# Two attention layers on one core: the residual input loaded three beats ahead, and the reciprocals of the first element at the end of their beat

## The chip, the core and the metric

The kernel runs on one core of one Trainium2 chip. The metric is the device time of one execution in microseconds (us); lower is better. The time before is the median of three runs. One more execution was recorded by the hardware profiler, and all durations below are from it. TensorE (PE) does the matrix products, VectorE (DVE), ScalarE (ACT) and GpSimd (POOL) the elementwise work, SyncE (SP) starts the transfers, in the order of its program. PEld in the profile is TensorE's loading of weights.

## The reference

Two graph layers over x, eight elements of 2048 rows of 256 features, with one 2048 x 2048 adjacency matrix for all. Cut to what matters:

```python
# layer 0: attention, softmax within each chunk of 256 keys, 4 heads of 64
q, k, v = (x @ Wq.T + bq), (x @ Wk.T + bk), (x @ Wv.T + bv)      # split into heads
scores = clip(q . k / sqrt(64), -10, 10)                          # b h n j c, j = chunk
scores = where(mask == 0, -10, scores)
attn = softmax(scores, axis=-1)                                   # over the 256 keys of a chunk
ctx = einsum('bhnjc,bhjcd->bhnd', attn, vc)                       # summed over 8 chunks
out = layernorm(ctx @ Wo.T + bo + x) * gamma + beta
h = layernorm(x + out)
# layer 1: graph attention
Wh = h @ W;  e = leaky_relu(Wh @ a1 [:, None] + Wh @ a2 [None, :], 0.2)
attention = softmax(where(mask, e, -inf))
result = layernorm(h + elu(attention @ Wh))
```

## The kernel before

**Blocks and beats.** The queries of an element are worked on in four blocks of 512 rows (`ib`), the keys in tiles of 128 (`c`, 16 a block); two tiles are a chunk (`j`, 8 a block). One tile of keys against one block of queries is a *beat*: 16 beats a block, 64 an element, 512 for layer 0 in all. The order of instructions on every engine is that of the program; nothing reorders them. Each beat has the same frame:

- `begin_beat` starts the steps of layer 1 for the element before (from the second element on): `low`, `weights`, `leaky`.
- The scores of layer 0 (`sc`, L892, TensorE), their clip and mask on VectorE (L903), their exponentials on ScalarE (`e`, L907).
- The products of the chunk before (L961, TensorE): in an even beat the sums of exponentials (`u<-e,ones`) and one half of the values, in an odd beat the other half. ScalarE copies the halves to `un` (L969) and the sums to `ds` (L975).
- `end_beat`: the products of layer 1 (`us`, L749), then one step of each generator that is alive, and functions that an agenda holds for this beat.

**The way of a denominator.** `ds` holds the sums once for each of 32 rows; a transfer takes one row of each head into a narrow tile `dc` (L977). `inverse` takes its reciprocal on VectorE (L983) and stores it to `rd` in DRAM (L985); `spread` loads it back, spread over the rows, as `r` (L989). `scaled` multiplies `un` by `r` on VectorE (L996; L994 for the first chunk), and GpSimd adds the product to `ctxT` (L997). In the first element `inverse` and `spread` come one beat after the sums, an odd beat, and `scaled` three beats later, an even one; from the second element on, all come one or two beats after the sums at the end of an even beat. `un` has two buffers (one more in turns in the first element), so ScalarE's next copy into it waits until GpSimd has read the one before.

**The finish of a block** is the generator `fin`, started by `scaled` of one of the last chunks. It loads the block's rows of x (`x`, 512 KB, L349), makes `y` = x + bo and adds beta to x on GpSimd (L352, L353), waits until the last chunk is in `ctxT`, and then takes a step a beat: the output projection `po` (L360, TensorE) added to `y` (L367), statistics (L319, L320, L324 and GpSimd's L325), normalization (L332), gamma and the sum with x (GpSimd, L373, L374), a second normalization, the store of h, and its transposition (L386). The beats of `fin` are counted here from the block's first: before the change the load is issued in beat 15 and the additions in beat 16 of the block, that is, beside the next block's first beats; `po` comes in beat 19, in the first element in beat 21.

**What else runs in the first element.** Generators stand in the list ahead of the `fin`s: `projections` (keys and values of the elements, `pk`, `pv`), `weights_made`, `masks_made` and `far_made`. `masks_made` loads pieces of the adjacency matrix (L145) and makes two 8-bit masks of each (L154, L157, with L161 on the diagonal, on VectorE; L155 on ScalarE), and stores them (L190, L191). `far_made` loads rows of the matrix (L197) and makes the row masks of layer 1 (L201, L204), stored by L205. The queries of the next block are projected (`xT_q`, L120; `pq`, L256) at the end of beats 11 and 13 of a block in the first element, 13 and 15 in the others.

**From the second element on** `prelude` prepares layer 1 of the element before, on top of its steps: products `pw` (L401), and the row maxima of masked sums, `half_max` (L441, VectorE, from `sj_row` and a row mask `fb` that is loaded by L433 into the buffer just read).

In `end_beat`, as long as the beat is of the first element (`2 * NIB * NCH` is 64), the agenda's functions other than `scaled` run before everything else.

## Time and profile before

| | |
|---|---|
| runs | 4379.75, 4382.11, 4390.98 us; median 4382.11 |
| profiled execution | 4383.33 us; span 4381.5 us; mean granted TensorE clock 0.98 |
| TensorE busy | 4049.8 us, 92% |
| VectorE busy | 3386.4 us, 77% |
| ScalarE busy | 2555.5 us, 58% |
| GpSimd busy | 1761.7 us, 40% |
| transfers | 415.63 MB; all but 4 MB from SyncE's queue |

How to read it: busy times are unions over the profiled execution; an engine may be busy at a lower rate than its best. A line of the waits gives the waiting engine and its line, what it waited for, then the time in total, the number of waits and the longest. A line of the timeline gives the start in us from the span's start, the duration, the engine, the line, the operation, output and inputs by name, the shape, and in brackets the engine's idle time before it and what ended that. A line of the stretches gives the stretch and its length, then the busy time (and instructions) of PE, PEld, DVE, ACT and POOL, the granted clock, the busy share of the DMA engines and GB/s. The one who released a wait is inferred and can be wrong where several things were waited for.

### The profile page before, as it was taken

The numbers are of one execution on the slowest core, as the hardware profiler recorded it, in microseconds if no ns is written. First come the engines' busy times: TensorE is split into PE (matmuls) and PEld (weight loads), VectorE is DVE, ScalarE is ACT, GpSimd is POOL, SyncE is SP. The second block draws the span as 40 slices with busy tenths as digits, with TensorE's granted clock in tenths as the row PEclk, the third lists the DMA queues.
The fourth block names the chain that finished last, engine by engine and source line by source line (L and its number), as shares of the span: only waits on it lengthen the run. The fifth ranks groups of instructions, "written<-read, shape, count | busy, mean of one in ns | idle before, by whom it ended". The sixth has DMA issues, their size and how long they took to land.

```text
span 4381.5 us, 61169 instructions
## 1 busy us (share of the span) xinstructions
PE 4049.8 (92%) x23053; PEld 1914.0 (44%) x23053; DVE 3386.4 (77%) x4530; ACT 2555.5 (58%) x3842; POOL 1761.7 (40%) x901
## 2 busy tenths in 40 slices
PE   8898989999999999999899998999989999899767
PEld 3233334453345534454344543445434454344456
DVE  5775589966898668976689766996589965888777
ACT  5665556655566555666456665666556665555546
POOL 0332235533445434544245442554335542344420
PEclk9999999999999999999999999999999999999889
DMA  5554232223332233322333223232232222422321
GB/s 170 184 175 146 76 105 85 81 69 100 100 91 78 59 107 98 100 73 61 99 97 97 73 75 107 85 94 78 71 107 88 83 79 67 119 83 78 126 69 58
DMA packets 257641, 415.63 MB, mean 95 GB/s; under 512 B 85440, under 2 KB 120512, under 8 KB 256448
## 3 DMA queue, kind: packets, MB, share of 16 engines
q1 hardware_dynamic: 257344, 411.71, 30.9%
q8 instruction: 181, 2.97, 0.3%
q14 instruction: 116, 0.95, 0.1%
HBM read 340.66 MB, written 68.88 MB: 93 GB/s over the span
## 4 chain that ended last, share of the span: by engine, by line
PE 60%; DVE 20%; ACT 8%; DMA 6%; issue 5%; POOL 1%; SPq 0%; DVEq 0%; ACTq 0%; POOLq 0%
PE u L961 18%; PE sc L892 15%; PE us L749 12%; DVE sc L903 5%; DVE w L721 3%; DVE fb L441 3%; DMA dc<-ds 3%; ACT e L907 3%; PE pk L256 3%; PE pv L275 2%; PE pq L256 2%; PE po L360 2%; DVE w L726 2%; PE pw L401 2%; PE us L764 1%
## 5 line engine op out<-in xcount | busy, mean ns | idle before, releaser
L903 DVE SCALAR_TENSOR_TENSOR sc<-sc,mk 128x1024 f32<-128x1024 f32 x1024 | 1206.6, 1223 | 535.6 <-PE sc L892 390.1
L907 ACT ACTIVATE e<-sc 128x1024 f32<-128x1024 f32 x1024 | 1033.2, 1021 | 934.9 <-DVE sc L903 909.8
L892 PE MATMUL sc<-qT,kT 64*128 64x512 f32 x4096 | 1038.1, 622 | 60.5 <-ACT e L907 57.0
L997 POOL TENSOR_TENSOR ctxT<-ctxT,un 128x1024 f32<-128x1024 f32 x224 | 561.6, 2507 | 1078.1 <-DVE un L996 1053.3
L961 PE MATMUL u<-e,v 128*32 128x512 f32 x8192 | 981.4, 597 | 0.0
L749 PE MATMUL us<-wh,w 128*128 128x256 f32 x3584 | 880.0, 395 | 91.3 <-ACT w L730 69.6
L749 PEld LDWEIGHTS us<-wh,w 128*128 128x128 f32 x3584 | 667.9, 193 | 433.1 <-ACT w L730 121.3
L739 POOL TENSOR_TENSOR acc<-acc,w 128x512 f32<-128x512 f32 x392 | 600.7, 1533 | 550.4 <-ACT w L730 540.0
L892 PEld LDWEIGHTS sc<-qT,kT 64*128 64x128 f32 x4096 | 345.3, 187 | 572.0 <-issue 319.0
L721 DVE SCALAR_TENSOR_TENSOR w<-ab,sj,w 128x512 f32<-128x512 f32 x512 | 578.1, 1150 | 5.7 <-ACT w L717 5.6
L961 PEld LDWEIGHTS u<-e,v 128*32 128x32 f32 x8192 | 240.5, 110 | 656.8 <-issue 504.2
L961 PE MATMUL u<-e,ones 128*32 128x512 f32 x4096 | 496.5, 603 | 0.0
L726 DVE TENSOR_TENSOR w<-w,mk 128x512 f32<-128x512 f32 x512 | 459.7, 919 | 44.1 <-DMA mk<-mask 41.5
L441 DVE CUSTOM_DVE_ANT_0 fb<-sj_row,fb 128x1024 bf16<-128x1024 f32 x240 | 379.8, 1593 | 5.6 <-DMA fb<-far 5.4
L969 ACT COPY un<-u 128x512 f32<-128x512 f32 x512 | 300.8, 588 | 125.5 <-PE u L961 96.9
L717 ACT ACTIVATE w<-ab,sj 128x512 f32<-128x512 f32 x512 | 352.3, 715 | 11.4 <-POOL acc L737 5.4
L730 ACT ACTIVATE w<-w 128x512 f32<-128x512 f32 x512 | 308.8, 629 | 82.7 <-DVE w L726 82.2
L996 DVE TENSOR_TENSOR un<-un,r 128x1024 f32<-128x1024 f32 x224 | 279.1, 1246 | 43.5 <-DMA r<-rd 36.8
L961 PEld LDWEIGHTS u<-e,ones 128*32 128x32 f32 x4096 | 107.3, 109 | 350.4 <-issue 281.9
L983 DVE RECIPROCAL dc<-dc 128x16 f32<-128x16 f32 x256 | 63.9, 250 | 161.3 <-DMA dc<-ds 149.0
L360 PE MATMUL po<-WT_o,ctxT 128*128 128x256 f32 x512 | 128.7, 408 | 36.4 <-POOL ctxT L997 35.5
L975 ACT COPY ds<-u 128x512 f32<-128x512 f32 x256 | 148.6, 580 | 17.6 <-PE u L961 16.0
(112 smaller groups left out, 3059.8 us busy)
## 6 DMA issues: line engine op xcount, KB each, us to landing
r<-rd SPq DMA_DIRECT2D x256, 256.0 KB
mk<-mask SPq DMA_DIRECT2D x120, 512.0 KB
fb<-far SPq DMA_DIRECT2D x240, 256.0 KB
xT_k<-in_xT_dram SPq DMA_DIRECT2D x32, 512.0 KB
raw<-in_adjT_dram SPq DMA_DIRECT2D x32, 512.0 KB
rawf<-in_adj_dram SPq DMA_DIRECT2D x32, 512.0 KB
x<-in_x_dram SPq DMA_DIRECT2D x32, 512.0 KB
h_d<-y SPq DMA_DIRECT2D x32, 512.0 KB
```

The source lines that it names most:

```text
L441: nc.vector.tensor_tensor_reduce(out=fb, in0=row, in1=fb, scale=1.0, scalar=2 * FAR * 0.999, op0=ALU.add, op1=ALU.max, accum_out=dst,)
L717: nc.scalar.activation(self.w, k["ab"][:, 1, :], AF.Identity, bias=k["sj"][:, 1, c : c + 1])
L721: nc.vector.scalar_tensor_tensor(self.w, k["ab"][:, 0, :], k["sj"][:, 0, c : c + 1], self.w, ALU.add, ALU.max)
L726: nc.vector.tensor_tensor(self.w, self.w, self.k["mks"][self.c // HT][:, self.c % HT, :], ALU.min)
L730: nc.scalar.activation(self.w, self.w, AF.Exp)
L739: nc.gpsimd.tensor_add(k["acc"], k["acc"], self.w)
L749: nc.tensor.matmul(k["us"][:, t, :], self.w[:, ts(t, P)], k["wh"][c // TPB][:, c % TPB, 0:F], start=(first and t % 2 == 0), stop=last, ski ...
L892: nc.tensor.matmul(sc[:, h, :], kTs[b][n // TPB][h * D : (h + 1) * D, hp, ts(n % TPB, P)], qTs[b, ib][h * D : (h + 1) * D, hp, :], start=True,
L903: nc.vector.scalar_tensor_tensor(sc, sc, -CLIP, cap, ALU.max, ALU.min)
L907: nc.scalar.activation(e, sc, AF.Exp)
L961: nc.tensor.matmul(m[h * DH : (h + 1) * DH, :], prev["v"][pc // TPB][:, pc % TPB, f0 : f0 + DH] if part < 2 else ones[:, 0:DH], prev["es"] ...
L997: nc.gpsimd.tensor_add(p["ctxT"], p["ctxT"], p["un"])
```

## The change

The load of x is issued two beats earlier in the block (the chunk whose `scaled` starts `fin` moves by one), and `fin` yields three times instead of once between load and additions, which so keep their beat. In `end_beat`, the part for the first element is dropped: `inverse` and `spread` now run where `scaled` runs, after the products and after all generators of the beat, in the order in which they were entered.

```diff
@@ fin
         xt = one.tile([P, TPB, F], F32, tag="x", name=f"x{b}_{ib}")
         nc.sync.dma_start(out=xt, in_=x[b, ts(ib, IB), :].rearrange("(t p) f -> p t f", p=P))
-        yield
+        for _ in range(3):
+            yield
         y = one.tile([P, TPB, F], F32, tag="y", name=f"y{b}_{ib}")
         nc.gpsimd.tensor_add(y, xt, bc_rows(bo_bc))
         nc.gpsimd.tensor_add(xt, xt, bc_rows(beta_bc))
@@ end_beat
         nonlocal weighted
-        if beat < 2 * NIB * NCH:
-
-            now = agenda.pop(beat, [])
-            agenda[beat] = [fn for fn in now if fn.__name__ == "scaled"]
-            for fn in now:
-                if fn.__name__ != "scaled":
-                    fn()
-        elif beat >= 2 * total:
+        if beat >= 2 * total:
             for fn in agenda.pop(beat, []):
                 fn()
         for s in weighted:
@@ scaled
-                            if p["j"] == NCH - (4 if p["b"] == 0 else 3):
+                            if p["j"] == NCH - (5 if p["b"] == 0 else 4):
                                 fins.append(fin(p["b"], p["ib"], p["ctxT"]))
```

## The prediction

> **What bounds the kernel now.** First the page: its span and the engines' busy line. Then the stretches, cut where an element begins (an element has 64 beats).

> ```profile
> span 4381.5 us, 61169 instructions
> PE 4049.8 (92%) x23053; PEld 1914.0 (44%) x23053; DVE 3386.4 (77%) x4530; ACT 2555.5 (58%) x3842; POOL 1761.7 (40%) x901
> ```
> ```profile
> 0.00:453.50 453.50, 409.24 (x2384) 147.40 (x2384) 298.04 (x407) 258.61 (x334) 110.29 (x52) 0.97 0.52 164
> 970.00:1498.00 528.00, 502.12 (x2887) 237.82 (x2885) 416.67 (x544) 314.50 (x477) 233.02 (x121) 0.99 0.29 87
> ```

> TensorE bounds nearly everything: in the third element it idles 528.0 - 502.1 = 26 us of 528. A change off TensorE can win only such idle time, so I looked for the stalls that the moved instructions cause. The waits, over the whole run and then over the first 453.5 us:

> ```profile
> POOL y L352 <- DMA x<-in_x_dram: 106.6, 9, 15.7
> PE po L360 <- POOL ctxT L997: 35.5, 15, 4.2
> ```
> ```profile
> ACT un L969 <- POOL ctxT L997: 24.0, 4, 12.5
> DVE dc L983 <- DMA dc<-ds: 26.4, 13, 5.2
> PE pk L256 <- ACT un L969: 10.2, 1, 10.2
> ```

> GpSimd waits for x, and what is queued behind its two additions is the addition into ctxT, for which ScalarE (the buffer of un) and TensorE (po) wait. The timeline at the last block of the first element shows the whole chain:

> ```profile
> 425.45 0.42 SPq L349 DMA_DIRECT2D x<-in_x_dram  x1
> 426.42 1.22 DVE L996 TENSOR_TENSOR un<-un,r 128x1024 f32<-128x1024 f32 x1
> 432.81 2.34 POOL L352 TENSOR_TENSOR y<-x,bo_bc 128x1024 f32<-128x1024 f32 x1 [11.31 <-DMA x<-in_x_dram]
> 435.22 2.34 POOL L353 TENSOR_TENSOR x<-x,beta_bc 128x1024 f32<-128x1024 f32 x1
> 437.52 2.34 POOL L997 TENSOR_TENSOR ctxT<-ctxT,un 128x1024 f32<-128x1024 f32 x1
> 439.89 0.59 ACT L969 COPY un<-u 128x512 f32<-128x512 f32 x1 [12.45 <-POOL ctxT L997]
> 440.53 3.73 PE L256 MATMUL pk<-xT_k,WT_k 128*128 128x512 f32 x4 [10.16 <-ACT un L969]
> ```

> The product un was ready at 427.6; its addition began at 437.5, behind x. The second effect is at the first block of the third element:

> ```profile
> 1078.52 2.36 POOL L352 TENSOR_TENSOR y<-x,bo_bc 128x1024 f32<-128x1024 f32 x1 [14.62 <-PE sc L892]
> 1080.01 1.96 DVE L441 CUSTOM_DVE_ANT_0 fb<-sj_row,fb 128x1024 bf16<-128x1024 f32 x1
> 1080.96 3.24 POOL L353 TENSOR_TENSOR x<-x,beta_bc 128x1024 f32<-128x1024 f32 x1
> 1081.90 3.39 DVE L441 CUSTOM_DVE_ANT_0 fb<-sj_row,fb 128x1024 bf16<-128x1024 f32 x1
> 1088.11 1.23 DVE L441 CUSTOM_DVE_ANT_0 fb<-sj_row,fb 128x1024 bf16<-128x1024 f32 x1 [0.54 <-DMA fb<-far]
> 1094.16 2.07 PE L360 MATMUL po<-WT_o,ctxT 128*128 128x256 f32 x4 [3.63 <-POOL ctxT L997]
> ```

> The row maximum takes 1.23 us alone, and 1.96 and 3.39 beside the two additions. (The name PE sc in the first line is wrong: the scores were long done; the transfers of x end at 1078.4.)

> **Part 1, x earlier.** The condition on j moves by one chunk (two beats) and two yields are added, so the additions keep their beat, 16 of a block, and the load goes from beat 15 to 13. Nothing is added but waiting room. The additions then start when GpSimd is through with the ctxT addition of beat 14.

> *First element, block 3.* That addition ends at 421.5, x landed long before (7.4 us from issue to use in the rows), so the additions run 421.5 to 426.2. There they meet L201 and L204 of the far rows (422.8, 423.5); the second comes free at 426.2, the clips go from 424.1 to 426.7, un from 426.4 to 429.1, the ctxT addition ends at 432.7, and the copy of un starts there instead of at 439.9: 7.1 us won. Ends: 5, and 10 for the whole stall.
> *Block 2.* The additions (322.6 to 327.4) stretched mask operations from 0.63 and 0.68 to 2.38 and 2.84 us, and TensorE stalled 1.40 + 0.78. At the new place, 311.4 to 316.2, they delay clips by 2.3 us, of which about 0.5 gets through to the scores of 318.3: 1.7 won.
> *Block 1.* Stalls of 1.19 + 1.31; at the new place (216.7 to 221.4) one L201 is late, 0.9 us, and the scores at 223.3 don't need it: 2.5 won. Blocks 1 and 2 together: 1 to 4.7.
> *Block 0.* Stalls of 1.65 + 0.75 = 2.4 go. But the new place, 120.6 to 125.3, is where beats 15 and 16 make masks: five operations without any slack in front of the clips at 122.8. Each addition holds up one of them by up to 2.2 us (2.84 - 0.68); the clips come 4 us late, of which I take 3.0 as a new stall: -0.6 (ends -2.5 and 2.4).
> Sum: 7.1 + 1.7 + 2.5 - 0.6 = 10.7.

> [...]

> *Elements 1 to 7, first block (7 times).* The additions move from 1078.5 to about 1063.9, where VectorE idles for 6.45 us waiting for scores. The row maxima shrink by (1.96 - 1.23) + (3.39 - 1.23) = 2.9 us. Then fb is late next: the third maximum waited 0.54 us for it already, and its load is issued only when the first maximum is done. So at least 0.7, at most 2.9 at po; the transfer of dc, no longer behind x, adds about 1 us in two of the seven (at 2139.2 and 3730.9 the reciprocal waited 3.9 and 4.1 us for it, against 2.2 in the third element). I take 1.9, between: 7 x 1.9 = 13.3. All TensorE stalls around these seven places add up to 35.
> *At nothing.* Second and fourth blocks: the additions wait for no x there (idle before them 0.0), GpSimd's queue sets their start. Third blocks: they start 3.7 us earlier and free 2.2 us of VectorE, but L602 then waits for pr of TensorE until 1329.4 as now; without that cover 1.3 a block would be won. x now leaves just ahead of xT_q, which has 17.3 us (1048.6 to 1065.9) for what takes about 7; SyncE's 0.45 us an issue lie in its waits for ds. The buffer of x was last read at least five beats earlier.

> **Part 2, the reciprocals.** In the first element's 31 odd beats the reciprocal L983, its store rd and the spread r went first in the beat; now they stand behind masks, projections, far rows and all their loads and stores, on VectorE and on SyncE's queue. Nothing is removed; what changes is who waits. VectorE waited 26.4 us for dc, 13 times, with masks behind. Where masks or far rows were behind such a wait (145.0, 192.1, 286.3, 337.1), the clips came 1.74, 1.76, 2.07 and 1.9 us later than they would with the masks in the wait, and TensorE stalls followed (0.58 and part of 1.94 at po; 2.69; 4.86; 0.98). I take 1.2 + 1.8 + 2.0 + 1.0 = 6.0, ends -2 and 9. On SyncE the loads of an odd beat no longer wait for rd and r, and leave some 3 to 7 us earlier. r leaves 2 to 3 us later: of block 1's beat 31 it left at 219.2 for a product at 236.5, so it has some 15 us; if that cover were gone, every us would go to un at 31 places. Where SyncE waits for rd, dc of the next beat is queued: 1.5 us of room (r at 123.5, dc at 125.6).

> **Sum.** 10.7 + 13.3 + 6.0 = 30.0. The profiled execution took 4383.3 us (span 4381.5), 1.2 over the median of the three runs, so 4353.3. Lower ends 5 + 1 - 2.5 - 2 + 5 = 6.5; upper 10 + 4.7 + 2.4 + 9 + 25 = 51.

> **Rivals.** A measurement of this kernel can tell 0.3%, 13 us.
> *The collisions only move* (0.18). The additions meet other operations at their new places and blocks 0 to 2 lose what they win; fb lets only 0.7 x 7 = 5 through; part 2 gives nothing. 7.1 + 5 - 4 = 8 won: 4375. For it: ten operations of VectorE stand at the four new places of the first element; against it: the idle 6.45 us in the later elements. [...]
> *All stalls go* (0.13): the upper ends, 51 won: 4332.
> *The reciprocal takes the clips with it* (0.14). It is now the last thing before the clips of the next beat, with no mask work left to fill a wait for dc. If SyncE, behind the stores that wait for masks, sends dc so late that the wait hits the clips in all 31 beats by 1.5 us, that is +46 against part 1's 24: 4406, slower. It decides from a dc later by more than the masks' own 2.6 us (120.3 to 122.9) plus the 1.5 us of room; against it, the loads ahead leave earlier.
> *Forecast* (0.55): 4353. Doing something else than it says I exclude: the beats follow from the code. Faster is forecast and upper rival, 0.68; same 0.18; slower 0.14. The range 4334 to 4376 leaves out the slow rival and the far end of the upper one.

> **What would show it.** GpSimd's wait for x near 0 instead of 106.6; the copy of un behind ctxT (24.0) down to some 8, with the 10.16 stall at about 3; row maxima of 1.2 us throughout at first blocks, and po's 35.5 at about 20; mask operations of over 2 us at beats 15 and 16 of block 0; L983's waits for dc in the first 64 beats well below 26.4. It is wrong if L903 waits for L983 beat after beat, if xT_q or fb become waits, or if the first element ends less than 10 us earlier than 453.5.

## The result, and the profile after

The changed kernel takes 4358.92 us (median of six runs, 4357.85 to 4361.75), the kernel before, beside it on the same chip, 4379.36 us (4376.92 to 4390.98). The ratio is 0.9949, with an interval of 0.9939 to 0.9960: faster by 20.4 us. The forecast was 30.0 us off the profiled execution, to 4353 (4334 to 4376). The sign and the range held, and so did the mechanism at the longest stall; the gain of elements 1 to 7 did not come, and the terms of the first element's other blocks are not borne out. The time is 6 us off, but the gain nearly 10: the 30.0 were taken off an execution 4 us above the median of before, which hid the rest by luck.

The profiled execution of the changed kernel took 4357.91 us. Of its page, the span and the engines; of its stretches, the first element and the third, cut again where an element begins:

```profile
span 4356.1 us, 61109 instructions
PE 4044.4 (93%) x23053; PEld 1915.6 (44%) x23053; DVE 3378.8 (78%) x4530; ACT 2556.2 (59%) x3842; POOL 1755.6 (40%) x901
```
```profile
0.00:436.20 436.20, 403.17 (x2388) 146.65 (x2389) 302.10 (x407) 257.84 (x334) 110.64 (x52) 0.99 0.53 170
950.80:1479.30 528.50, 502.26 (x2887) 237.88 (x2885) 416.54 (x544) 314.84 (x477) 230.82 (x121) 0.99 0.29 87
```

The first element is 17.3 us shorter (436.2 for 453.5), and in it the granted clock rose from 0.97 to 0.99. The third element, where the forecast expected 1.9 us, is no shorter: 528.5 for 528.0. The two spans differ by 25.4 us, 5 more than the medians, because the one profiled execution of before lies 4 us above its median and that of the change 1 below; stretches of single profiles are read with that in mind. (A second profile of the change, taken with later runs, has a first element of 444.6 us, only 8.9 shorter.)

The waits, over the whole run (three lines) and then over the first element, 0 to 436.2 us (two lines):

```profile
PE po L361 <- POOL ctxT L991: 44.9, 17, 5.1
DVE fb L442 <- DMA fb<-far: 22.0, 8, 3.8
DVE dc L977 <- DMA dc<-ds: 140.7, 104, 4.7
```
```profile
DVE dc L977 <- DMA dc<-ds: 19.5, 10, 4.5
ACT un L963 <- POOL ctxT L991: 3.2, 1, 3.2
```

GpSimd's wait for x (106.6 us before) has no line any more. The copy of un behind ctxT fell from 24.0 to 3.2 us in the first element. But TensorE's wait for ctxT at `po` rose from 35.5 to 44.9, and VectorE's wait for `fb` came up from 5.4 to 22.0 us: of the prediction's own signs of being wrong, "if xT_q or fb become waits" has come for `fb`.

The timeline at the last block of the first element, the chain that the prediction showed:

```profile
395.89 0.90 SPq L349 DMA_DIRECT2D x<-in_x_dram  x1
...
412.99 2.37 POOL L353 TENSOR_TENSOR y<-x,bo_bc 128x1024 f32<-128x1024 f32 x1
414.18 1.73 DVE L201 TENSOR_SCALAR mf<-rawf 128x1024 bf16<-128x1024 int32 x1
415.44 2.70 POOL L354 TENSOR_TENSOR x<-x,beta_bc 128x1024 f32<-128x1024 f32 x1
415.95 2.27 DVE L204 TENSOR_TENSOR mf<-mf,off_h 128x128 bf16<-128x128 bf16 x1
...
420.56 1.21 DVE L990 TENSOR_TENSOR un<-un,r 128x1024 f32<-128x1024 f32 x1
421.91 2.34 POOL L991 TENSOR_TENSOR ctxT<-ctxT,un 128x1024 f32<-128x1024 f32 x1 [3.76 <-DVE un L990]
424.28 0.59 ACT L963 COPY un<-u 128x512 f32<-128x512 f32 x1 [3.24 <-POOL ctxT L991]
424.92 1.98 PE L256 MATMUL pk<-xT_k,WT_k 128*128 128x512 f32 x4 [1.84 <-ACT un L963]
```

x is issued 17 us before its additions, for a transfer that took 7.4 us before; nothing waits for it. The additions meet L201 and L204 as forecast (1.73 and 2.27 us long), and GpSimd is idle again when the product un comes. The stall of 10.16 us has become 1.84.

The first block of the third element, where two effects were to be seen, a gain and what comes after it:

```profile
1045.27 2.35 POOL L353 TENSOR_TENSOR y<-x,bo_bc 128x1024 f32<-128x1024 f32 x1
1047.70 2.34 POOL L354 TENSOR_TENSOR x<-x,beta_bc 128x1024 f32<-128x1024 f32 x1
1060.61 0.46 SPq L140 DMA_DIRECT2D mk<-mask  x1
1060.85 1.21 DVE L442 CUSTOM_DVE_ANT_0 fb<-sj_row,fb 128x1024 bf16<-128x1024 f32 x1
1061.99 1.22 DVE L442 CUSTOM_DVE_ANT_0 fb<-sj_row,fb 128x1024 bf16<-128x1024 f32 x1
1062.10 1.47 SPq L434 DMA_DIRECT2D fb<-far  x2
1069.05 1.23 DVE L442 CUSTOM_DVE_ANT_0 fb<-sj_row,fb 128x1024 bf16<-128x1024 f32 x1 [3.56 <-DMA fb<-far]
1072.70 2.34 POOL L991 TENSOR_TENSOR ctxT<-ctxT,un 128x1024 f32<-128x1024 f32 x1 [13.44 <-DVE un L990]
1075.10 6.46 PE L361 MATMUL po<-WT_o,ctxT 128*128 128x256 f32 x16 [4.67 <-POOL ctxT L991]
```

The gain is there: the row maxima take 1.21 and 1.22 us where they took 1.96 and 3.39. And it is lost again in the line of the third maximum, which waits 3.56 us for its rows `fb`, where it waited 0.54. The stall at `po` is 4.67 us, longer than the 3.63 of before. Just ahead of `fb` on the queue, at 1060.61, stands the load `mk` of the masks of layer 0, 512 KB.

### The profile page after: what moved, and what is told of

Read it like the earlier page. It is cut to its first block, busy times and chain, and to the rows that moved or that the text cites. A ratio compares the mean times of both kernels' runs of the same rounds, so it can differ in the third digit from the quotient of the medians.

```text
span 4356.1 us, 61109 instructions
## 1 busy us (share of the span) xinstructions
PE 4044.4 (93%) x23053; PEld 1915.6 (44%) x23053; DVE 3378.8 (78%) x4530; ACT 2556.2 (59%) x3842; POOL 1755.6 (40%) x901
## 3 DMA queue, kind: packets, MB, share of 16 engines
q1 hardware_dynamic: 257344, 411.71, 30.9%
## 4 chain that ended last, share of the span: by engine, by line
PE 58%; DVE 22%; ACT 7%; DMA 6%; issue 5%; POOL 1%; SPq 0%; DVEq 0%; ACTq 0%; POOLq 0%
PE u L955 18%; PE sc L886 14%; PE us L750 12%; DVE sc L897 6%; DVE w L722 3%; DVE fb L442 3%; PE pk L256 3%; PE pv L275 3%; ACT e L901 2%; DMA dc<-ds 2%; PE po L361 2%; PE pq L256 2%; PE pw L402 2%; DVE w L727 2%; PE us L765 1%
## 5 line engine op out<-in xcount | busy, mean ns | idle before, releaser
L750 PEld LDWEIGHTS us<-wh,w 128*128 128x128 f32 x3584 | 667.5, 193 | 426.4 <-ACT w L731 114.7
L722 DVE SCALAR_TENSOR_TENSOR w<-ab,sj,w 128x512 f32<-128x512 f32 x512 | 591.2, 1176 | 5.8 <-ACT w L718 5.8
L727 DVE TENSOR_TENSOR w<-w,mk 128x512 f32<-128x512 f32 x512 | 441.4, 883 | 45.0 <-DMA mk<-mask 42.5
L718 ACT ACTIVATE w<-ab,sj 128x512 f32<-128x512 f32 x512 | 352.2, 714 | 10.7 <-POOL acc L738 5.5
L361 PE MATMUL po<-WT_o,ctxT 128*128 128x256 f32 x512 | 133.9, 420 | 45.8 <-POOL ctxT L991 44.9
L969 ACT COPY ds<-u 128x512 f32<-128x512 f32 x256 | 148.5, 580 | 15.0 <-PE u L955 13.7
```

Source lines behind the costliest of these rows:

```text
L718: nc.scalar.activation(self.w, k["ab"][:, 1, :], AF.Identity, bias=k["sj"][:, 1, c : c + 1])
L722: nc.vector.scalar_tensor_tensor(self.w, k["ab"][:, 0, :], k["sj"][:, 0, c : c + 1], self.w, ALU.add, ALU.max)
L727: nc.vector.tensor_tensor(self.w, self.w, self.k["mks"][self.c // HT][:, self.c % HT, :], ALU.min)
L750: nc.tensor.matmul(k["us"][:, t, :], self.w[:, ts(t, P)], k["wh"][c // TPB][:, c % TPB, 0:F], start=(first and t % 2 == 0), stop=last, ski ...
```

## The experiments

Theory: the first element wins what its terms say, and elements 1 to 7 win little, since `fb` waits behind `mk`. Rivals: the parts are mis-sized in the first element; or `fb` is late because its load is issued late, whatever stands ahead of it.

**Only x earlier.** `end_beat` stays as before.

```diff
-        if beat >= 2 * total:
+        if beat < 2 * NIB * NCH:
+            now = agenda.pop(beat, [])
             ...
+        elif beat >= 2 * total:
```

> Only the early load of x (with the chunk that starts fin); the reciprocals of the first element stay first in their beat. Theory (the parts add up, as the prediction summed them): the whole change won 20 us by the medians, of which the reciprocals are 6, so this kernel is about 14 us faster than before, ratio 0.9967, and the stall of 10 us at the last block of the first element is gone here too. Rival (the load alone does it all): the whole 20 us, ratio 0.995. Second rival (the early load needs the later reciprocals, since raw loads hold up x): x still arrives late at GpSimd and no more than 5 us are won.

Measured: 4365.28 us against 4379.11, ratio 0.9971 (0.9961 to 0.9981), 13.8 us won, as expected. The 10-us stall is gone here too. From the sums of exponentials (`u<-e,ones`) of beat 64 to those of beat 66, across the stall, TensorE gains 9.0 us on the kernel before. But it starts those of beat 64 4.4 us later than the kernel before, so the first element is only 4.6 us shorter in this profile (448.9 for 453.5).

**Only the reciprocals later.** `fin` and its start stay as before.

```diff
-        for _ in range(3):
-            yield
+        yield
...
-   if p["j"] == NCH - (5 if p["b"] == 0 else 4):
+   if p["j"] == NCH - (4 if p["b"] == 0 else 3):
```

> Only the reciprocals behind the beat's other work in the first element; x is loaded one beat ahead of its additions as before. Theory: 6 us faster than before (ratio 0.9986); the clips after masks come earlier by 1.7 to 2.1 us where VectorE waited for dc, and the stall of 10 us behind x stays. Rival (the reciprocal takes the clips with it, dc late in every odd beat): slower by up to 20 us, ratio 1.005. Second rival (hidden anyway): 0 +- 2 us.

Measured: 4363.95 us, ratio 0.9963 (0.9950 to 0.9975), 15.2 us won, far over the 6.0 of the prediction. The timeline at the last block of the first element, with the code of x unchanged, shows what the 6.0 had left out:

```profile
416.82 0.43 SPq L349 DMA_DIRECT2D x<-in_x_dram  x1
420.91 2.35 POOL L352 TENSOR_TENSOR y<-x,bo_bc 128x1024 f32<-128x1024 f32 x1 [6.58 <-DMA x<-in_x_dram]
...
428.00 0.59 ACT L962 COPY un<-u 128x512 f32<-128x512 f32 x1 [7.74 <-POOL ctxT L990]
428.64 3.78 PE L256 MATMUL pk<-xT_k,WT_k 128*128 128x512 f32 x4 [5.44 <-ACT un L962]
```

x, too, is loaded in an odd beat, by a generator, so it too now goes ahead of `rd` and `r` on SyncE. The stall is 5.44 us instead of 10.16. Both parts take from the same stall: across it TensorE gains 9.0 us with the early x alone, 3.8 with the reciprocals alone and 8.9 with both, so that 3.9 us are counted twice when the parts are added up. Alone the parts win 13.8 + 15.2 = 29.0 by the medians, together 20.4; the other 4.7 us of the difference lie within the intervals of the medians (each some 5 us to either side). Added to the first part, the second wins 4365.3 - 4358.9 = 6.4, close to the prediction's 6.0, but good to some 6 us only.

**x earlier in the first element alone,** both parts of the change there, the later elements as before:

```diff
-        for _ in range(3):
+        for _ in range(3 if b == 0 else 1):
...
-   if p["j"] == NCH - (5 if p["b"] == 0 else 4):
+   if p["j"] == NCH - (5 if p["b"] == 0 else 3):
```

> The change, but x is loaded three beats ahead in the first element only; from the second element on it is loaded one beat ahead, as before. Theory after reading the changed kernel's trace (the leads of TensorE grow by 4 us in all over the first blocks of elements 1 to 7): this kernel is 4 to 8 us slower than the full change, so 12 to 16 us faster than before, ratio 0.9968. Rival (the prediction's term): 13.3 us slower than the full change, ratio 0.998.

Measured: 4362.93 us, ratio 0.9962 (0.9950 to 0.9975), 16.2 us won. The prediction had 10.7 + 6.0 = 16.7 for just this. In its profile the first element itself is 12.2 us shorter (441.3). For the elements 1 to 7 it leaves 4362.9 - 4358.9 = 4 us, where 13.3 was forecast; by the two intervals (each some 5 us to either side) the 4 is good to about 7.

**The mask loads of layer 0 two beats later.** The change, with the load of `mk` moved out of the way of `fb`:

```diff
-                if c % HT == 1:
+                if c % HT == 3:
```

> The change, and the loads of layer 0's mask blocks (512 KB, in beats 1 and 9 of a block) are issued two beats later, in beats 3 and 11, so that in the first block of an element they no longer stand ahead of the row masks fb. Theory (fb is held up by the mask load ahead of it on the same DMA rings): VectorE's wait of 3.6 us for fb at the first blocks falls below 1.5 us, po's stall there from 4-5 to 2-3 us, and the kernel is 8 to 16 us faster than the change, ratio 0.992 to before. Rival (fb is held up by r, the spread of the reciprocals, which lands on few of the rings, or by its own length): the wait stays within 1 us and so does the time.

Measured: 4318.06 us, ratio 0.9859 (0.9846 to 0.9873), 41 us below the change itself, where 8 to 16 were expected. The timeline at the same first block of the third element:

```profile
1058.55 1.22 DVE L442 CUSTOM_DVE_ANT_0 fb<-sj_row,fb 128x1024 bf16<-128x1024 f32 x1
1058.66 1.47 SPq L434 DMA_DIRECT2D fb<-far  x2
1062.62 1.22 DVE L442 CUSTOM_DVE_ANT_0 fb<-sj_row,fb 128x1024 bf16<-128x1024 f32 x1 [0.56 <-DMA fb<-far]
1068.68 3.72 PE L361 MATMUL po<-WT_o,ctxT 128*128 128x256 f32 x16 [1.69 <-POOL ctxT L991]
1068.72 0.47 SPq L140 DMA_DIRECT2D mk<-mask  x1
```

With `mk` behind it, `fb` is used 3.96 us after its issue (1058.66 to 1062.62); with `mk` ahead it took 6.95 us (1062.10 to 1069.05). The issue is not late, the transfer is: this separates the theory from its rival. The stall at `po` falls from 4.67 to 1.69.

**What early x is worth once the masks are out of the way.** The same one-line edit on the version with early x in the first element alone, and on the kernel before, and the change once more beside them (these three against 4379.41; the 4362.9 and the 4318.1 of the table are from above, against 4379.11):

> Mask loads two beats later, as in mask_two_beats_later, but x loaded three beats ahead in the first element only. Theory (the 13.3 us that the prediction put on the first blocks of elements 1 to 7 were swallowed by the wait for fb, and appear once fb is there in time): 10 to 14 us slower than mask_two_beats_later's 4318, so 4328 to 4332, ratio 0.989. Rival (an earlier x is worth 4 us there whatever fb does): 4322, ratio 0.987.

> The kernel before with nothing but the mask loads two beats later. Theory (early x and a free fb need each other in the later elements, the rest of the mask loads' gain is their own): the change is worth more on top of it than on top of the kernel before, 28 to 32 us instead of 20, so this runs in 4347 to 4350, ratio 0.993. Rival (independent): 41 us faster than before, 4338, ratio 0.9906.

> The change itself, beside the kernels of this call. The medians of its two parts alone, 13.8 and 15.2 us, add up to 29, the whole had won 20.4. Theory (in the first element the parts add up, 4.6 and 11.0 us of lead against 17.4 together, and the excess of the medians is scatter between runs): 20 us again, ratio 0.9954. Rival (the first measurement of the whole was low): 27 to 29 us, ratio 0.9935.

| early x | masks as they were | masks two beats later |
|---|---|---|
| nowhere (kernel before) | 4379.4 | 4354.2 (ratio 0.9942, 0.9929 to 0.9954) |
| first element only, with the reciprocals | 4362.9 | 4342.3 (0.9914, 0.9901 to 0.9926) |
| everywhere (the change) | 4358.9 (0.9953, 0.9941 to 0.9966) | 4318.1 (0.9859, 0.9846 to 0.9873) |

The change wins 20.5 us again, so its first measurement was not low. The other two miss what was expected of them: 4342.3 for 4328 to 4332, and 4354.2 for 4347 to 4350. Down the right column, early x in elements 1 to 7 is worth 4342.3 - 4318.1 = 24 us (good to some 8); down the left one, 4.

The traces show that this happens at the seven first blocks. Take from each later element the stretch from the first product of the sums in beat 14 to that in beat 26, and add up the seven; in it, take TensorE's waits at the scores (`sc`) for ScalarE's exponentials, and at `po` for ctxT (all in us, one profile each):

| kernel | stretch | wait at `sc` | wait at `po` |
|---|---|---|---|
| before | 542.4 | 24.5 | 24.5 |
| only the reciprocals later | 533.3 | 21.3 | 21.1 |
| x early in the first element only | 536.7 | 24.1 | 21.8 |
| only x earlier | 534.0 | 12.9 | 29.9 |
| the change | 538.0 | 13.6 | 30.5 |
| the change once more | 537.9 | 13.5 | 30.9 |
| before, masks later | 532.6 | 23.5 | 19.5 |
| x early in the first element only, masks later | 536.1 | 26.1 | 17.9 |
| the change, masks later | 513.2 | 12.6 | 15.0 |
| the change, third buffer | 526.1 | 13.6 | 24.2 |
| the change, both | 509.8 | 13.2 | 11.1 |

With the masks as they were, early x takes some 10 us off the wait at `sc` and puts most of it back at `po`; the stretch is as long as without. With the masks later it is some 20 us shorter. So the gain is real, and in the change it is used up by the wait for `fb`. Of the 41 us of the later masks, 24.8 lie in these stretches, and 13.7 in beats 26 to 38 (721.9 to 708.2), where the kernel before gains much the same from the masks alone (721.1 to 710.3).

With the masks later but x late, the maxima stand beside the additions again (x only in the first element early, third element):

```profile
1063.28 2.01 DVE L442 CUSTOM_DVE_ANT_0 fb<-sj_row,fb 128x1024 bf16<-128x1024 f32 x1
1065.21 3.39 DVE L442 CUSTOM_DVE_ANT_0 fb<-sj_row,fb 128x1024 bf16<-128x1024 f32 x1
1076.84 5.41 PE L361 MATMUL po<-WT_o,ctxT 128*128 128x256 f32 x16 [2.99 <-POOL ctxT L991]
```

Either delay alone keeps the stall: 2.99 us with the stretched maxima, 4.67 with the late `fb`, 1.69 with neither.

**A third buffer for `fb`,** so that its load can be issued earlier, once on the change and once with the masks later as well (`ds` gives up one of its two buffers for the room):

```diff
-                fb = two.tile([P, HN], BF16, tag="fb", ...)
+                fb = three.tile([P, HN], BF16, tag="fb", ...)
...
-        load()
-        load()
+        for _ in range(3):
+            load()
...
-                        ds = two.tile([P, IB], F32, tag="ds", ...)
+                        ds = one.tile([P, IB], F32, tag="ds", ...)
```

> The change with three buffers for the row masks fb and three loads at once at the start (ds has one buffer instead of two to make room). The mask load stays ahead of the fourth fb. Theory: the third row maximum no longer waits, the fourth still does, as its load is issued no earlier and lands at the same time; VectorE's wait of 3.6 us at the first blocks moves to the fourth maximum and shrinks by one maximum, 1.2 us; 0 to 8 us faster than the change, ratio 0.994 to 0.995. Rival (a third buffer is all that is missing): wait gone, as much won as with the mask loads two beats later, ratio 0.988.

> The change with both: mask loads two beats later and three buffers for fb (ds with one). Theory (both take away the same wait for fb at the first blocks, of which the mask loads' shift already leaves 0.5 us): little on top of mask_two_beats_later's 4318, 4310 to 4320, ratio 0.985. Rival (each frees a part of its own, 40 and 16 us): about 4302, ratio 0.9825.

Measured: 4342.62 us (ratio 0.9914, 0.9900 to 0.9927) on the change, 4310.05 us (0.9843, 0.9827 to 0.9860, against 4376.55) with both, the best version of this study. The first wins 16 us on the change, where 0 to 8 were expected; at the first block of its third element the third maximum has no wait and the fourth one of 1.49 us, as expected. The waits over the whole run, of the version with both:

```profile
DVE fb L442 <- DMA fb<-far: 1.8, 2, 1.4
PE po L361 <- POOL ctxT L991: 22.2, 16, 2.5
```

The two waits over the kernels, in us, each from its profile:

| kernel | VectorE for `fb` | TensorE at `po` | mean granted clock |
|---|---|---|---|
| before | 5.4 | 35.5 | 0.980 |
| the change | 22.0 | 44.9 | 0.982 |
| x early in the first element only | 3.7 | 33.1 | 0.983 |
| the change, third buffer | 13.8 | 38.0 | 0.984 |
| before, masks later | 1.4 | 30.8 | 0.983 |
| x early in the first element only, masks later | 1.4 | 27.0 | 0.983 |
| the change, masks later | 6.4 | 26.4 | 0.986 |
| the change, both | 1.8 | 22.2 | 0.985 |

**The collision in block 0.** The prediction put the additions of the very first block among the mask operations, for a new stall of 3.0 us. In the change's timeline it is there:

```profile
117.52 2.85 DVE L157 TENSOR_SCALAR mb<-raw 128x1024 int8<-128x1024 int32 x1
119.89 2.70 POOL L354 TENSOR_TENSOR x<-x,beta_bc 128x1024 f32<-128x1024 f32 x1
120.40 2.54 DVE L161 TENSOR_TENSOR mb<-mb,off_h 128x128 int8<-128x128 int8 x2
123.63 2.33 DVE L897 SCALAR_TENSOR_TENSOR sc<-sc,mk 128x1024 f32<-128x1024 f32 x2
125.94 1.13 PE L886 MATMUL sc<-qT,kT 64*128 64x512 f32 x4 [2.36 <-ACT e L901]
...
131.06 1.13 PE L886 MATMUL sc<-qT,kT 64*128 64x512 f32 x4 [1.07 <-ACT e L901]
```

To see what it costs in the end, x of that one block was loaded as late as before:

```diff
-        for _ in range(3):
+        for _ in range(1 if (b, ib) == (0, 0) else 3):
...
-   if p["j"] == NCH - (5 if p["b"] == 0 else 4):
+   if p["j"] == NCH - (4 if (p["b"], p["ib"]) == (0, 0) else 5 if p["b"] == 0 else 4):
```

> The change, but the very first block (element 0, block 0) loads its x one beat ahead of the additions, as before. Theory (the earlier additions hold up the masks of beats 15 and 16 there, the prediction's -0.6 for this block): the stalls of 2.36 and 1.07 us near 126 and 131 us go, and TensorE reaches beat 18 three to five us earlier than in the change; with part of it given back by beat 24, where the old place collides with L201 and L204 again (stall of about 2.9 us near 147, as with the reciprocals alone). Rival (the stall at 126 us comes from the later reciprocals): it stays.

Measured, in a single execution: 4353.18 us. Its timeline at the same place:

```profile
119.28 0.68 DVE L157 TENSOR_SCALAR mb<-raw 128x1024 int8<-128x1024 int32 x1
121.17 2.33 DVE L897 SCALAR_TENSOR_TENSOR sc<-sc,mk 128x1024 f32<-128x1024 f32 x2
125.61 2.98 POOL L353 TENSOR_TENSOR y<-x,bo_bc 128x1024 f32<-128x1024 f32 x1 [6.80 <-DMA x<-in_x_dram]
```

The stretched L157 is 0.68 us again, and the clips start 2.46 us earlier (121.17 for 123.63). Measured by the start of the same products of sums, TensorE gains 4.0 us there on the change (from 1.8 us behind it to 2.2 ahead) and is 0.1 us ahead at beat 24, after a stall of 3.0 us at 147 where the change has 1.4. So the collision is real, and some 2 us of it remain. A single execution can't tell the 5 us in the total from scatter.

## Why the prediction was right, and where not

- **First element, early x: 10.7.** Right at its largest term, not shown in the others, and as a total in part luck. The 7.1 at block 3 has its row: ScalarE's copy comes 15.6 us earlier (424.28 for 439.89), of which TensorE had 8.5 already at the sums of beat 64, so 7.1 were won here. TensorE won 8.9, since the products behind the old stall had run slowly (`pk` in 3.73 us, now 1.98), which the sum had no term for. Blocks 0 to 2 were to win 1.7 + 2.5 - 0.6 = 3.6; with early x alone TensorE is 4.4 us behind the kernel before at the end of them, 1.9 of it from before the first of the additions. Block 0 was forecast with a new stall of 3.0 and has 2.36 + 1.07 = 3.4; in the net it costs some 2 us, not 0.6. L157 took 2.85 us there beside the addition and 0.68 with x late.
- **The first element as a whole: 16.7.** The version that changes it alone wins 16.2 (by its interval 10.9 to 21.9). But five profiles have the same program in the first element (the change and once more, x early there only, and the two with x early and the masks later), and it is shorter by 17.3, 8.9, 12.2, 13.0 and 14.9 us there: 16.7 lies at the upper end. Nor is it all idle time, which is all that the prediction counted ("can win only such idle time"): of the 17.3, TensorE's busy time gave 6.1 (409.24 to 403.17 us), at a granted clock of 0.99 for 0.97. Its idle time fell from 44.3 us to between 31.0 and 37.7.
- **The reciprocals: 6.0.** Agrees on top of the early x (6.4), but 15.2 when done alone. What the text left out is in its own sentence "the loads of an odd beat no longer wait for `rd` and `r`": x is one of those loads, and nothing was put down for it. In the sum that did no harm, since the same stall is counted once in the first part. Place by place the term is not shown: in the one profile of the reciprocals alone, TensorE gains 2.6 us around 192.1 (forecast 1.8), but around 145.0, 286.3 and 337.1 it loses 2.0, 1.1 and 0.1. The waits for dc in the first element fell from 26.4 to 19.5 in the change (21.9 in its second profile), but are 28.6 with the reciprocals alone, 6.1 of it in one wait at the stall. The slow rival, dc late for the clips in every odd beat, did not come: there are 10 waits in the change, the largest 4.5 us.
- **Elements 1 to 7: 7 x 1.9 = 13.3.** Wrong in size: 4, and nothing that can be told from scatter at the seven places themselves. The gain of 2.9 us at the maxima is there in full. The step that failed is the value taken, "1.9, between" the ends 0.7 and 2.9. The rows of before already spoke for the lower end: `fb` was issued at 1082.00, when the first maximum was done, and its maximum began at 1088.11, the moment it had landed, 6.1 us later. Of the gain, then, only the 0.73 us of the first maximum could bring the landing forward; the 2.16 of the second could only become a wait, and did (0.54 to 3.56, the transfer itself 0.8 us longer). Seven times 0.7 is 4.9, and 4 was measured. At this step the rival "the collisions only move" was right, with its "fb lets only 0.7 x 7 = 5 through". What held `fb` was the load of the masks in front of it (6.95 us from issue to use with it there, 3.96 with it behind), which the prediction did not cost. (The upper end of 25 is not worked out there either: 7 x 2.9 is 20.3.)
- **The view that said so.** The prediction expected po's 35.5 at about 20. It is 44.9. With the masks out of the way it is 26.4, and with the third buffer too 22.2.
- **What the sum had no term for.** The clock: TensorE's busy time fell by 5.4 us with the same 23053 products, and the fall is that of the first element.

What stays open: the spans of the change and of the change with the masks later differ by 42.0 us. TensorE's busy time accounts for 15.2 of it (4044.4 to 4029.2, the same products), the wait at `po` for 18.5 (44.9 to 26.4); the remaining 8 are idle time elsewhere that was not followed, and why beats 26 to 38 gain is not shown. The third buffer alone shortens the span by 15.2 us, of which `po` shows 6.9 and the busy time 4.9. Whether `ds` with one buffer has an effect of its own in it was not tried.

## What to carry to other kernels

When a stretched operation is freed, look at what the next wait would be if nothing were stretched: when its load is issued, how long that takes with the loads ahead of it on the queue (6.95 us here behind `mk`, 3.96 ahead of it), and so the earliest time the freed engine can go on. Two delays that end at nearly the same time hide each other, so one edit alone shows almost nothing (4 us here), and the same edit shows its whole worth once the other delay is gone (24 us). And a load moved past other instructions takes its neighbours on the queue along: cost each of them.

## What the runs showed of the hardware

**The stall at `po` was paid twice.** Stretches of the change, around the `po` of the third element; the column after GpSimd's is TensorE's granted clock:

```profile
1070.50:1075.00 4.50, 0.00 (x0) 0.00 (x0) 4.50 (x7) 1.12 (x2) 2.29 (x1) 0.87 0.42 118
1075.00:1078.40 3.40, 3.30 (x8) 2.67 (x9) 2.28 (x4) 1.31 (x2) 0.05 (x1) 0.50 0.36 94
```

and with the masks two beats later:

```profile
1062.00:1077.00 15.00, 13.31 (x88) 5.82 (x84) 13.30 (x26) 4.76 (x7) 3.37 (x2) 1.00 0.50 130
```

After 4.5 us without a product TensorE ran at half clock for the next 3.4 us, and the 16 products of `po` took 6.46 us; after the stall of 1.69 us the clock stayed at 1.00 and they took 3.72. In the version with early x in the first element only and the masks later, a stall of 2.99 us (to 1076.84) was followed by a stretch at 0.62, and `po` took 5.41 us:

```profile
1073.40:1076.80 3.40, 0.45 (x7) 0.00 (x0) 3.40 (x5) 1.18 (x2) 2.34 (x1) 1.00 0.46 132
1076.80:1080.20 3.40, 3.36 (x10) 2.73 (x11) 2.44 (x5) 1.25 (x2) 0.00 (x0) 0.62 0.62 161
```

The stall of 4.67 us so cost 6.46 - 3.72 = 2.7 us more at `po`.

But the length of a stall did not decide by itself. In the change TensorE stalled 2.36 us ahead of products of `sc` (to 125.94) and 2.38 us ahead of products of `pw` (to 2079.35); behind the first the clock stayed at 1.00, behind the second it was 0.50:

```profile
126.00:132.00 6.00, 4.93 (x28) 1.26 (x28) 5.13 (x8) 4.83 (x7) 2.35 (x1) 1.00 0.62 166
2080.80:2084.20 3.40, 3.40 (x9) 2.11 (x9) 0.00 (x0) 1.13 (x4) 0.00 (x0) 0.50 0.56 169
```

```profile
121.54:124.95 3.41, 2.04 (x16) 0.37 (x8) 3.41 (x6) 0.09 (x1) 1.05 (x1) 1.00 0.16 61
124.95:128.36 3.41, 2.42 (x20) 0.72 (x20) 3.38 (x6) 3.41 (x5) 0.00 (x0) 1.00 0.16 45
2077.38:2080.79 3.41, 1.44 (x7) 1.27 (x8) 1.51 (x2) 2.05 (x4) 0.00 (x0) 1.00 0.26 54
```

So in these traces half clock went with the share of idle time within one window, and not with the length of a stall alone: of 114 stalls of 2.8 to 3.1 us in the first 3850 us, 83 were followed by half clock.
